# A second kept path of 544 tokens beside the one of 576 in a masked attention with residual

## The chip, the cores and the metric

The kernel runs on one core of a Trainium2 chip. The metric is the device time of one execution in microseconds (us). Three runs of the kernel before gave 808.4, 808.93 and 811.0 us; the median is 808.93 us.

In the profile, PE is TensorE (PEld its weight loads), DVE is VectorE, ACT is ScalarE, POOL is GpSimd and SP is the engine that issues most transfers. A "q" behind an engine's name (DVEq) means its instruction queue: branches, register loads and waits stand there.

## The reference

The input x has 8 batches of 512 features by 1024 tokens. A mask of 8 x 1024 ones and zeros says which tokens are kept. Each batch goes through one attention layer with 8 heads of 64 features, and its output is added to x:

```python
q = xt @ Wq.T                                  # queries, keys and values are the same
scores = scale * einsum('bhqd,bhkd->bhqk', qh, qh)
logits = (scores * cmask + (1.0 - cmask) * NEG) * rmask
attn = softmax(logits, axis=-1)
ctx = einsum('bhqk,bhkd->bhqd', attn, qh)
out = ctx @ Wo.T
x = x + transpose(out)
```

A masked key gets no weight. A masked query has all logits 0, so that its result is the mean of all values: one and the same row for all masked queries of a batch. The drawn mask keeps 505, 529, 523, 514, 519, 519, 533 and 521 tokens in the eight batches.

## The kernel before

**Two paths.** The kernel first ranks the kept tokens of each batch (`early`). `verdict` holds the largest number of kept tokens in any batch. Each engine loads it into a register (line 1255) and compares (line 1256): if it is below NK = 576, the short path (`late`) runs, which works on NK packed tokens a batch. Its column NK - 1 holds the mean token, which stands for all masked queries. After that path each engine loads `flag` (line 1259) and jumps over the general path for all 1024 tokens (line 1260), unless the short path was not taken or found a sum that vanishes.

**The packed tokens.** `gather` fetches the kept rows of x (turned to tokens by features and stored in DRAM as xd) by an indirect DMA on POOL's queue, five chunks a batch: four of 128 tokens and a last one of 64 (`sizes`, LAST = 4). `collect` turns them on TensorE into xc, with features on the partitions (line 527).

**Pairs.** The work goes by 32 pairs: 8 batches times 4 pairs of heads. For pair p the loop over the chunks c = 0 to 4 does this:

- `scores`: s = keys of the chunk times all queries, in two halves of KH = 288 queries for two heads (line 627), then the exponential e on ScalarE (line 631). In the last chunk of 64 keys the two halves of the queries share the 128 partitions.
- `add_up`: VectorE sums e over the valid queries (line 648). The scores are symmetric, so these sums are the softmax denominators.
- tasks for other pairs, put between the chunks by hand (`slots_of` and the tables TURN, SEARCH, LATER, FINISH): `project` of pair p + 2 (pq, line 558), `values` of pair p + 2 (transposes v, line 577, and the squared lengths, lines 585 to 594), `bias_of` of pair p + 1, the output projection of the batch before (`output`, line 777), `collect` of the next batch, transposes and searches of the next batch, and the last steps of an earlier one.

After the chunks, `attend` multiplies e with v (av, line 664). `invert` sends the sums through DRAM to get them as a row over all partitions (rb), and `contexts` multiplies. The order in which the code calls these functions is the order of the instructions on each engine; no scheduler moves them.

**The last chunk.** qT is 640 columns wide. Columns 576 to 639 are a copy of the last 64 (line 567), so that the last chunk also has 128 rows. In `output`, the last chunk of 64 rows is computed in two halves of 256 features, which lie in partitions 0 to 63 and 64 to 127 of one bank; two DMAs on POOL's queue store them (line 786).

**Homes.** At its end the kernel needs, for every token, the row of the packed output that belongs to it (`origin`; `placed` is the same as floats). `early` computes it from the ranks with five VectorE instructions (lines 1060 to 1065, tiles `home` and `wrap`), a transpose on TensorE (`home_t`, line 1077) and two copies (lines 1078 and 1079). `place_blocks`, in pair 2, chunk 2, makes `block_origin` of it (line 830).

**The end.** The last batch goes a shorter way (`begin_output`, `end_output`, `attend_last`, `fetch_last`, `finish_tokens`), and ACT's queue issues the last stores (line 897).

Of the kernel before, what the change touches and what calls it, by code (L numbers as in the profile page):

```python
# [11 lines left out]
I32 = mybir.dt.int32  # L12
# [9 lines left out]
Q = 32  # L22
NK = 576
TINY = 1e-26
# [3 lines left out]
def attention_of_all_tokens(ctx, tc, x, mask, out, ident, wqT, woT):  # L28

# [275 lines left out]
def attention_of_kept_tokens(ctx, tc, x, mask, wq, wo, out, ident, wqT, woT, verdict, flag):  # L319

    nc = tc.nc
# [10 lines left out]
    NQ = 4  # L355
    KH = NK // 2
    sizes = [min(P, NK - c * P) for c in range(-(-NK // P))]
    NC = len(sizes)
    LAST = NC - 1
    assert sizes[LAST] == DK == P // 2  # L360
    W = NC * P

    sb = ctx.enter_context(tc.tile_pool(name="fsb", bufs=2))
# [3 lines left out]

    count = keep.tile([P, NK], F32, name="count")
    quadrant = keep.tile([P, A], F32, name="quadrant")
# [10 lines left out]
    sums = [keep.tile([P, 2, NC], F32, name=f"sums_{i}") for i in range(2)]  # L380
    ris = [keep.tile([P, Q], F32, name=f"ris_{i}") for i in range(2)]
    ranks = dr.tile([B * NT, P], F32, name="ranks", bufs=1)

# [19 lines left out]
    def queries_of(b):  # L403

        valid = sb.tile([P, NK], F32, tag="valid", name=f"valid_{b}")
        nc.gpsimd.tensor_scalar(valid, count, kept[:, b : b + 1], None, ALU.is_lt)  # L406
        part = sb.tile([P, KH], F32, tag="part", name=f"part_{b}")
        for r in range(2):
            rows = slice(r * DK, (r + 1) * DK)
            nc.gpsimd.tensor_copy(part[rows, :], valid[rows, r * KH : (r + 1) * KH])  # L410
        valids[b] = valid, part

    def turn_first(i):

        r, at = divmod(i * P, NB)
        pt = bank(f"xt_0_{i}")
        for d in range(ND):
            nc.tensor.transpose(pt[:, d * P : (d + 1) * P], xs[0][r][:, d, at : at + P], ident)  # L418
        if i == 0:
            xds[0] = dr.tile([T, D], F32, tag="xd", name="xd_0")  # L420
        tag = "oc" if i < NC else "xin"
        xt = sb.tile([P, D], F32, tag=tag, name=f"xt_0_{i}", bufs=NC)
        nc.scalar.copy(
            xt.rearrange("p (a d f) -> p a d f", a=A, d=ND),
            pt.rearrange("p (d a f) -> p a d f", d=ND, a=A),
        )
        nc.gpsimd.dma_start(xds[0][i * P : (i + 1) * P, :], xt)

    def mean_first():
        xbars[0] = sb.tile([P, ND, NN], F32, tag="xbar", name="xbar_0")  # L430
        for r in range(NN):
            nc.vector.tensor_reduce(xbars[0][:, :, r], xs[0][r], axis=AX.X, op=ALU.add)

    def turn(b, i):

        n = T // NQ
        r, at = divmod(i * n, NB)
        if i == 0:
            xds[b] = dr.tile([T, D], F32, tag="xd", name=f"xd_{b}")
        xt = sb.tile([P, n // Q, P], F32, tag="xt", name=f"xt_{b}_{i}", bufs=2)
        nc.vector.transpose(  # L447
            xt.rearrange("p k (d f) -> p k d f", d=ND),
            xs[b][r][:, :, at : at + n].rearrange("p d (k t) -> p k d t", t=Q),
        )  # L450

        def store():
            for a in range(A):
                to = xds[b][i * n : (i + 1) * n, a * P : (a + 1) * P]
                nc.sync.dma_start(
                    to.rearrange("(k t) c -> t k c", t=Q), xt[a * Q : (a + 1) * Q, :, :]
                )

        stores[1].append(store)
# [20 lines left out]
    def place_ranks(b):  # L480
        rank = sb.tile([P, T], F32, tag="rank", name=f"rank_{b}", bufs=1)
        found = sb.tile([P, NC], F32, tag="found", name=f"found_{b}")
        source = sb.tile([P, NC], I32, tag="source", name=f"source_{b}")
        searches[b] = rank, found, source
# [8 lines left out]
    def search(b, i):  # L493

# [52 lines left out]
    def project(pair, hf):  # L549
# [16 lines left out]
        if hf == 1:  # L566
            nc.scalar.copy(qT[:, NK:W], pq[:, KH - DK : KH])

# [41 lines left out]
    def scores(pair, c):  # L610
        qT, nm = qTs[pair], "%d_%d_%d" % (*pair, c)
        heads = [slice(h * DK, (h + 1) * DK) for h in range(2)]
        keys = slice(c * P, c * P + sizes[c])
        if c < LAST:
# [133 lines left out]
    def sum_last(pair):  # L748

        rb = rbs[pair]  # L750
        end = rb[:, NK - DK : NK]
        nc.vector.tensor_tensor(end, end, rb[:, NK:W], ALU.add)
        nc.vector.tensor_tensor(lowest, lowest, end, ALU.min)
        nc.vector.tensor_scalar(end, end, TINY, None, ALU.max)
        nc.vector.reciprocal(end, end)
# [8 lines left out]
    ods, gs, xrs = {}, {}, {}  # L764
    places = [slice(DK + c * P, DK + (c + 1) * P) for c in range(LAST)] + [slice(0, DK)]

    def output(b, i):
# [4 lines left out]
        oc = sb.tile([P, D], F32, tag="oc", name=f"oc_{b}_{i}", bufs=NC)  # L772
        parts = 2 if i == LAST else 1
        w = D // parts
# [87 lines left out]
    def fetch_last(b):  # L862

        for i in range(NT):
            tag, bufs = ("xin", NC) if i < NC else ("g", NT)
            g = sb.tile([P, D], F32, tag=tag, name=f"g_{b}_{i}", bufs=bufs)
            rows = min(NK, DK + (i + 1) * P)
            nc.gpsimd.indirect_dma_start(
# [100 lines left out]
    def early():  # L969
# [11 lines left out]
        def where(t, src, pattern, op, base, mult):  # L981
# [13 lines left out]
            count,  # L995
            pattern=[[1, NK]],
            base=0,
# [33 lines left out]
        nc.scalar.copy(rank, pr[:BC, :P])  # L1031
        nc.gpsimd.dma_start(ranks, rank)

        place_ranks(0)
# [23 lines left out]

        home = keep.tile([BC, P], F32, name="home")
        nc.vector.tensor_scalar(home, rank, float(-NK), None, ALU.add)  # L1060
        nc.vector.tensor_tensor(home, home, mrow, ALU.mult)
        nc.vector.tensor_scalar(home, home, float(NK - 1 + DK), None, ALU.add)
        wrap = keep.tile([BC, P], F32, name="wrap")
        nc.vector.tensor_scalar(wrap, home, float(NK), float(-NK), ALU.is_ge, ALU.mult)
        nc.vector.tensor_tensor(home, home, wrap, ALU.add)
        nc.vector.memset(low, 1.0)
# [7 lines left out]
        for i in range(NC):  # L1074
            search(0, i)
        pt = bank("home_t")
        nc.tensor.transpose(pt[:, :BC], home, ident[:BC, :BC])
        nc.vector.tensor_copy(placed, pt[:, :BC].rearrange("p (b c) -> p b c", c=NT))
        nc.vector.tensor_copy(origin, placed)

    def late():
        weights["wq"] = order_columns(load_weights(wq, "wq"), "wq")
# [33 lines left out]
        for p, pair in enumerate(pairs):  # L1116
# [3 lines left out]
            for c in range(NC):  # L1120
# [36 lines left out]
                if pr == 2 and c == 0 and b > 0:  # L1157
                    fetch(b - 1)
                if p == 2 and c == 2:
                    place_blocks()  # L1160
# [60 lines left out]
def kernel(  # L1221
# [9 lines left out]

    nc = tc.nc
# [11 lines left out]
    with ExitStack() as pools:  # L1249
        early, late = attention_of_kept_tokens(  # L1250
            pools, tc, x, mask, wq, wo, out, ident, wqT, woT, verdict, flag
        )
        with tc.manual_schedule():
            early()
        fit = nc.values_load(verdict[0:1, 0:1], min_val=0, max_val=2 * T)
        with tc.If(fit < NK):
            with tc.manual_schedule():
                late()
    again = nc.values_load(flag[0:1, 0:1], min_val=0, max_val=1)
# [31 lines left out]
```

## Time and profile before

| what | value |
|---|---|
| median of the runs | 808.93 us |
| span of the profiled execution | 724.6 us |
| own time of the profiled execution beyond its span | not shown |
| median less span | 84.3 us |
| PE, DVE, ACT, POOL busy | 673.4, 542.0, 384.1, 171.9 us |
| one steady batch (av of one pair to the same av of the next batch) | 83.02 us |
| mean granted clock of TensorE | 0.980 |

The page of the profile gives busy times, the chain of work that ended last, and groups of instructions by line. A row of a group reads: line, engine, operation, tile written <- tiles read, shapes, count | busy us, mean ns of one | idle time of the engine just before them, and who ended it. A matmul in float32 counts as two instructions. Matmuls overlap, so the mean of one is longer than the distance from one to the next; the timeline gives the distance. A row of the timeline reads: start in us, length in us, engine, line, operation, tiles, shape, count, and in brackets the wait before it. A row of the table by stage reads: from:to, length, busy us of PE, PEld, DVE, ACT and POOL with counts, the granted clock of TensorE, the busy share of the DMA engines, and GB/s. A row of the view of one source line gives the shortest, median and longest duration in ns and the start of the first and the last in us.

### The profile page before, as it was taken

The numbers are of one execution on the slowest core, as the hardware profiler recorded it, in microseconds if no ns is written. First come the engines' busy times: TensorE is split into PE (matmuls) and PEld (weight loads), VectorE is DVE, ScalarE is ACT, GpSimd is POOL, SyncE is SP. The second block draws the span as 40 slices with busy tenths as digits, with TensorE's granted clock in tenths as the row PEclk, the third lists the DMA queues.
The fourth block names the chain that finished last, engine by engine and source line by source line (L and its number), as shares of the span: only waits on it lengthen the run. The fifth ranks groups of instructions, "written<-read, shape, count | busy, mean of one in ns | idle before, by whom it ended". The sixth has DMA issues, their size and how long they took to land.

```text
span 724.6 us, 11742 instructions
## 1 busy us (share of the span) xinstructions
PE 673.4 (93%) x4027; PEld 378.0 (52%) x4027; DVE 542.0 (75%) x1568; ACT 384.1 (53%) x763; POOL 171.9 (24%) x208
## 2 busy tenths in 40 slices
PE   6699999999999999999999999999999999998973
PEld 5555555555554555546554555455554555554332
DVE  6269967758986799858986699858988598637862
ACT  5476567455654556445664657445673645445300
POOL 4721000062102601054101701044100710023021
PEclk9899999999999999999999999999999999999985
DMA  8544152772579636783579634785468821754238
GB/s 292 157 150 129 56 164 64 185 196 93 181 199 234 201 96 181 209 207 124 164 193 229 200 125 142 206 222 152 164 169 199 215 88 41 167 132 131 59 113 248
DMA packets 96405, 117.35 MB, mean 162 GB/s; under 512 B 10080, under 2 KB 73632, under 8 KB 96336
## 3 DMA queue, kind: packets, MB, share of 16 engines
q1 hardware_dynamic: 79584, 74.14, 38.9%
q0 software_dynamic: 12528, 40.28, 17.8%
q10 hardware_dynamic: 4224, 2.10, 1.0%
q8 instruction: 33, 0.54, 0.3%
q14 instruction: 36, 0.29, 0.1%
HBM read 73.30 MB, written 43.18 MB: 161 GB/s over the span
## 4 chain that ended last, share of the span: by engine, by line
PE 82%; DVE 7%; ACT 6%; DMA 3%; issue 2%; POOL 0%; SPq 0%; DVEq 0%; POOLq 0%
PE av L664 19%; PE s L627 19%; PE pq L558 17%; PE po L777 15%; ACT e L631 4%; PE v L577 3%; PE xc L527 2%; DVE junk L648 2%; PE pa L797 2%; DVE junk L502 1%; DMA g<-od,origin 1%; PE xt L418 1%; DMA rb<-row 1%; PE po L813 1%; PE top L600 0%
## 5 line engine op out<-in xcount | busy, mean ns | idle before, releaser
L648 DVE CUSTOM_DVE_ANT_0 junk<-e,valid 128x576 f32<-128x576 f32 x256 | 193.5, 756 | 68.3 <-ACT e L631 61.3
L627 PE MATMUL s<-qT 64*128 64x288 f32 (+1 forms) x1280 | 186.7, 434 | 16.9 <-ACT e L631 16.7
L631 ACT ACTIVATE e<-s,bias 128x576 f32<-128x576 f32 x256 | 175.5, 737 | 20.4 <-PE s L627 17.2
L627 PEld LDWEIGHTS s<-qT 64*128 64x128 f32 (+1 forms) x1280 | 91.7, 174 | 103.9 <-ACT e L631 50.2
L558 PE MATMUL pq<-xc,wqT 128*128 128x288 f32 x512 | 140.4, 418 | 0.0
L664 PE MATMUL av<-e,v 128*64 128x288 f32 x1024 | 135.8, 411 | 0.1
L558 PEld LDWEIGHTS pq<-xc,wqT 128*128 128x128 f32 x512 | 92.2, 190 | 40.9 <-ACT cT L680 8.5
L777 PE MATMUL po<-woT,cT 128*128 128x512 f32 (+1 forms) x336 | 113.4, 525 | 0.0
L664 PEld LDWEIGHTS av<-e,v 128*64 128x64 f32 x1024 | 69.6, 136 | 55.0 <-ACT v L580 8.3
L786 POOL DMA_DIRECT2D od<-oc x42 | 23.4, 557 | 276.0 <-ACT oc L784 276.0
L777 PEld LDWEIGHTS po<-woT,cT 128*128 128x128 f32 (+1 forms) x336 | 48.9, 172 | 56.0 <-issue 51.5
L680 ACT COPY cT<-av 128x288 f32<-128x288 f32 x62 | 21.7, 402 | 97.7 <-PE av L664 97.7
L879 POOL DMA_INDIRECT g<-od,block_origin x56 | 62.1, 1109 | 19.0 <-issue 14.3
L784 ACT COPY oc<-po 128x512 f32<-128x512 f32 (+1 forms) x35 | 19.0, 543 | 87.0 <-PE po L777 85.7
L565 ACT COPY qT<-pq 128x288 f32<-128x288 f32 x64 | 25.5, 398 | 63.8 <-PE pq L558 63.8
L514 POOL DMA_INDIRECT xin<-xd,source x40 | 42.4, 1060 | 43.8 <-DVE m L603 25.6
L406 POOL TENSOR_SCALAR valid<-count,kept 128x576 f32<-128x576 f32 x8 | 14.1, 1762 | 130.3 <-DVE sums L648 130.2
L447 DVE STREAM_TRANSPOSE xt<-x 128x1024 f32<-128x1024 f32 x28 | 34.7, 1240 | 11.0 <-DMA xd<-xt 10.9
L587 DVE TENSOR_REDUCE len<-sq 128x10 f32<-128x640 f32 x32 | 25.8, 806 | 21.3 <-ACT sq L585 21.3
L502 DVE TENSOR_SCALAR_CACHE_REDUCE junk<-rank,key 128x1024 f32<-128x1024 f32 (+4 forms) x40 | 39.7, 994 | 1.5 <-ACT rank L1046 1.5
L849 DVE TENSOR_TENSOR xr<-o,xr 128x512 f32<-128x512 f32 x56 | 38.8, 692 | 1.9
L846 DVE STREAM_TRANSPOSE o<-g 128x512 f32<-128x512 f32 x56 | 39.3, 701 | 0.0
(139 smaller groups left out, 630.5 us busy)
## 6 DMA issues: line engine op xcount, KB each, us to landing
x<-in_x_dram SPq DMA_DIRECT2D x56, 256.0 KB
xd<-xt SPq DMA_DIRECT2D x112, 128.0 KB
xr<-in_x_dram SPq DMA_DIRECT2D x28, 512.0 KB
out_dram<-xr SPq DMA_DIRECT2D x24, 512.0 KB
rb<-row SPq DMA_DIRECT2D x60, 160.0 KB
od<-oc POOLq DMA_DIRECT2D x28, 256.0 KB, 4.0
rank<-ranks SPq DMA_DIRECT2D x6, 512.0 KB
xd<-xt POOLq DMA_DIRECT2D x8, 256.0 KB, 3.8
```

The lines of the kernel that those rows point to most:

```text
L447: nc.vector.transpose(xt.rearrange("p k (d f) -> p k d f", d=ND), xs[b][r][:, :, at : at + n].rearrange("p d (k t) -> p k d t", t=Q),)
L502: nc.vector.tensor_scalar(junk[:, :n], rank[:, i * P :], key[:, col], 0.0, ALU.is_le, ALU.add, accum_out=found[:, col])
L514: nc.gpsimd.indirect_dma_start(out=xin[:n, :], out_offset=None, in_=xds[b], in_offset=bass.IndirectOffsetOnAxis(ap=searches[b][2][:n, i : ...
L558: nc.tensor.matmul(pq[:, :KH], wqT[:, d, pr * P : (pr + 1) * P], xcs[b][:, d, cols], start=(d == 0), stop=(d == ND - 1),)
L627: nc.tensor.matmul(s[to, h, :KH], qT[heads[h], keys], qT[heads[h], queries], start=True, stop=True)
L631: nc.scalar.activation(e[:, hf if c < LAST else 0, :, :], s[:, :, :KH], AF.Exp, bias=biases[pair][:, c : c + 1], scale=SCALE,)
L648: nc.vector.tensor_tensor_reduce(junk[:, :n].rearrange("p (f k) -> p f k", k=KH), e[:, :, h, :], (valid if c < LAST else part).rearrange(" ...
L664: nc.tensor.matmul(av[head, :KH], v[keys, c, head], e[keys, hf if c < LAST else 0, h, :], start=(c == 0), stop=(c == LAST),)
L777: nc.tensor.matmul(po[k * n : (k + 1) * n, :w], cTs[b, pr][:, i * P : i * P + n], woT[:, pr, k * w : (k + 1) * w], start=(pr == 0), stop=( ...
L846: nc.vector.transpose(o.rearrange("p k t -> p (k t)"), gs[b, i])
L849: nc.vector.tensor_tensor(to, o, to, ALU.add)
L879: nc.gpsimd.indirect_dma_start(out=g, out_offset=None, in_=ods[b], in_offset=bass.IndirectOffsetOnAxis(ap=block_origin[:, b, i : i + 1], a ...
```

## The change

A second length, SHORT = 544, gets its own copy of the short path. `late` now takes the length and sets NK, KH, the chunk sizes and the places of the output rows by `fit_to`; its code stands twice in the program. With NK = 544 a half has 272 queries, the last chunk has END = 32 tokens, qT's columns 544 to 639 are three copies of the last 32, and the last chunk of an output is computed in four quarters of 128 features with four stores. The `home` instructions depend on NK, so they leave `early` and become `place_all`, called in pair 1, chunk 4, ahead of that chunk's tasks. xd, the feature sums and the source rows of batch 0 get buffers of their own, since both copies read them.

```diff
-NK = 576
+SHORT = 544
+LONG = 576
...
+    def fit_to(n):
+        nonlocal NK, KH, END
+        NK, KH, END = n, n // 2, n - LP
+        assert DK % END == 0
+        sizes[:] = [P] * LAST + [END]
+        places[:] = [slice(END + c * P, END + (c + 1) * P) for c in range(LAST)] + [slice(0, END)]
...
-            xds[0] = dr.tile([T, D], F32, tag="xd", name="xd_0")
+            xds[0] = dr.tile([T, D], F32, tag="xd_0", name="xd_0", bufs=1)
...
-            nc.scalar.copy(qT[:, NK:W], pq[:, KH - DK : KH])
+            nc.scalar.copy(
+                qT[:, NK:W].rearrange("p (r k) -> p r k", k=END),
+                pq[:, KH - END : KH].unsqueeze(1).to_broadcast([P, (W - NK) // END, END]),
+            )
...
-        keys = slice(c * P, c * P + sizes[c])
+        keys = slice(c * P, c * P + (P if c < LAST else DK))
...
-        end = rb[:, NK - DK : NK]
-        nc.vector.tensor_tensor(end, end, rb[:, NK:W], ALU.add)
+        end = rb[:, LP : LP + DK]
+        nc.vector.tensor_tensor(end, end, rb[:, LP + DK : W], ALU.add)
...
-        parts = 2 if i == LAST else 1
+        parts = P // n
...
-        home = keep.tile([BC, P], F32, name="home")
-        nc.vector.tensor_scalar(home, rank, float(-NK), None, ALU.add)
-        nc.vector.tensor_tensor(home, home, mrow, ALU.mult)
-        nc.vector.tensor_scalar(home, home, float(NK - 1 + DK), None, ALU.add)
-        wrap = keep.tile([BC, P], F32, name="wrap")
-        nc.vector.tensor_scalar(wrap, home, float(NK), float(-NK), ALU.is_ge, ALU.mult)
-        nc.vector.tensor_tensor(home, home, wrap, ALU.add)
...
+    def place_all():
+
+        BC = B * NT
+        mrow, rank = seen["mrow"], seen["rank"]
+        home, wrap = homes
+        nc.vector.tensor_scalar(home, rank, float(-NK), None, ALU.add)
+        nc.vector.tensor_tensor(home, home, mrow, ALU.mult)
+        nc.vector.tensor_scalar(home, home, float(NK - 1 + END), None, ALU.add)
+        nc.vector.tensor_scalar(wrap, home, float(NK), float(-NK), ALU.is_ge, ALU.mult)
+        nc.vector.tensor_tensor(home, home, wrap, ALU.add)
         pt = bank("home_t")
         nc.tensor.transpose(pt[:, :BC], home, ident[:BC, :BC])
         nc.vector.tensor_copy(placed, pt[:, :BC].rearrange("p (b c) -> p b c", c=NT))
         nc.vector.tensor_copy(origin, placed)
 
-    def late():
+    def late(n):
+        fit_to(n)
...
+                if p == 1 and c == 4:
+                    place_all()
                 if p == 2 and c == 2:
                     place_blocks()
...
-        with tc.If(fit < NK):
+        with tc.If(fit < SHORT) as short:
             with tc.manual_schedule():
-                late()
+                late(SHORT)
+        with short.Else():
+            with tc.If(fit < LONG):
+                with tc.manual_schedule():
+                    late(LONG)
```

More of the change, by code (lines that the diff above doesn't have):

```diff
@@ L355, in attention_of_kept_tokens @@
     NQ = 4
-    KH = NK // 2
-    sizes = [min(P, NK - c * P) for c in range(-(-NK // P))]
-    NC = len(sizes)
+    NC = -(-LONG // P)
     LAST = NC - 1
-    assert sizes[LAST] == DK == P // 2
+    LP = LAST * P
     W = NC * P
+    assert LP < SHORT < LONG == LP + DK and DK == P // 2
+    NK = KH = END = 0
+    sizes, places = [], []
+    def fit_to(n):
[4 more added lines that the diff above has]
+        places[:] = [slice(END + c * P, END + (c + 1) * P) for c in range(LAST)] + [slice(0, END)]
     sb = ctx.enter_context(tc.tile_pool(name="fsb", bufs=2))
@@ L366, in attention_of_kept_tokens @@
     keep = ctx.enter_context(tc.tile_pool(name="keep", bufs=1))
-    count = keep.tile([P, NK], F32, name="count")
+    count = keep.tile([P, LONG], F32, name="count")
     quadrant = keep.tile([P, A], F32, name="quadrant")
@@ L381, in attention_of_kept_tokens @@
     ris = [keep.tile([P, Q], F32, name=f"ris_{i}") for i in range(2)]
+    homes = [keep.tile([B * NT, P], F32, name=f"home_{i}") for i in range(2)]
+    seen = {}
     ranks = dr.tile([B * NT, P], F32, name="ranks", bufs=1)
@@ L405, in queries_of @@
         valid = sb.tile([P, NK], F32, tag="valid", name=f"valid_{b}")
-        nc.gpsimd.tensor_scalar(valid, count, kept[:, b : b + 1], None, ALU.is_lt)
+        nc.gpsimd.tensor_scalar(valid, count[:, :NK], kept[:, b : b + 1], None, ALU.is_lt)
         part = sb.tile([P, KH], F32, tag="part", name=f"part_{b}")
@@ L429, in mean_first @@
     def mean_first():
-        xbars[0] = sb.tile([P, ND, NN], F32, tag="xbar", name="xbar_0")
+        xbars[0] = keep.tile([P, ND, NN], F32, name="xbar_0")
         for r in range(NN):
@@ L482, in place_ranks @@
         found = sb.tile([P, NC], F32, tag="found", name=f"found_{b}")
-        source = sb.tile([P, NC], I32, tag="source", name=f"source_{b}")
+        if b:
+            source = sb.tile([P, NC], I32, tag="source", name=f"source_{b}")
+        else:
+            source = keep.tile([P, NC], I32, name="source_0")
         searches[b] = rank, found, source
@@ L764, in attention_of_kept_tokens @@
     ods, gs, xrs = {}, {}, {}
-    places = [slice(DK + c * P, DK + (c + 1) * P) for c in range(LAST)] + [slice(0, DK)]
     def output(b, i):
@@ L866, in fetch_last @@
             g = sb.tile([P, D], F32, tag=tag, name=f"g_{b}_{i}", bufs=bufs)
-            rows = min(NK, DK + (i + 1) * P)
+            rows = min(NK, END + (i + 1) * P)
             nc.gpsimd.indirect_dma_start(
@@ L995, in early @@
             count,
-            pattern=[[1, NK]],
+            pattern=[[1, LONG]],
             base=0,
@@ L1032, in early @@
         nc.gpsimd.dma_start(ranks, rank)
+        seen["mrow"], seen["rank"] = mrow, rank
         place_ranks(0)
```

## The prediction

> **What bounds the kernel now.** I read the page first: its span, the busy times, and the chain that ended last.
>
> ```profile
> span 724.6 us, 11742 instructions
> PE 673.4 (93%) x4027; PEld 378.0 (52%) x4027; DVE 542.0 (75%) x1568; ACT 384.1 (53%) x763; POOL 171.9 (24%) x208
> PE 82%; DVE 7%; ACT 6%; DMA 3%; issue 2%; POOL 0%; SPq 0%; DVEq 0%; POOLq 0%
> ```
>
> TensorE is busy for 93% of the span and carries 82% of the chain. The median of the runs is 808.93 us, so 84.3 us lie around the span; the profiled execution shows nothing of them, and I add changes of the span to the median. Next came the groups of instructions with shapes kept apart (count | busy us, mean ns), because the change alters shapes.
>
> ```profile
> L648 DVE CUSTOM_DVE_ANT_0 junk<-e,valid 128x576 f32<-128x576 f32 x256 | 193.5, 756 | 68.3 <-ACT e L631 61.3
> L627 PE MATMUL s<-qT 64*128 64x288 f32 x1024 | 163.8, 435 | 9.2 <-ACT e L631 9.0
> L558 PE MATMUL pq<-xc,wqT 128*128 128x288 f32 x512 | 140.4, 418 | 0.0
> L664 PE MATMUL av<-e,v 128*64 128x288 f32 x1024 | 135.8, 411 | 0.1
> L777 PE MATMUL po<-woT,cT 128*128 128x512 f32 x224 | 100.3, 595 | 0.0
> L648 DVE CUSTOM_DVE_ANT_0 junk<-el,part 128x288 f32<-128x288 f32 x64 | 29.0, 454 | 2.9 <-ACT el L631 1.7
> L565 ACT COPY qT<-pq 128x288 f32<-128x288 f32 x64 | 25.5, 398 | 63.8 <-PE pq L558 63.8
> L784 ACT COPY oc<-po 128x512 f32<-128x512 f32 x28 | 16.4, 585 | 77.9 <-PE po L777 77.9
> L527 PE MATMUL xc<-ident,xin 64*128 64x64 f32 x32 | 3.7, 235 | 0.0
> ```
>
> Every 288 here becomes 272 and every 576 becomes 544, if the new path is taken. The stage that repeats eight times is a batch, and one batch in the table of busy times by stage reads (engine busy us, matmuls in brackets):
>
> ```profile
> 253.21:336.23 83.02, 80.57 (x487) 44.36 (x488) 67.47 (x193) 46.57 (x95) 20.80 (x22) 1.00 0.65 177
> ```
>
> PE works 80.57 of 83.02 us and DVE 67.47, so in a steady batch PE is the bound and the other engines have slack. The spacing of its work is read from the timeline, from one group's start to the next.
>
> ```profile
> 285.75 4.10 PE L664 MATMUL av<-e,v 128*64 128x288 f32 x32
> 289.78 0.72 PE L664 MATMUL av<-el,v 64*64 64x288 f32 x8
> 290.43 1.24 PE L627 MATMUL s<-qT 64*128 64x288 f32 x8
> 291.60 2.21 PE L558 MATMUL pq<-xc,wqT 128*128 128x288 f32 x8
> 293.64 3.60 PE L777 MATMUL po<-woT,cT 128*128 128x512 f32 x8
> 297.17 1.24 PE L627 MATMUL s<-qT 64*128 64x288 f32 x8
> ```
>
> **Part 1, narrower queries (a gain on PE).** A pq of 288 columns takes (293.64-291.60)/8 = 255 ns, a po of 512 columns (297.17-293.64)/8 = 441 ns: 0.83 ns a column. From busy time, 100.3/224 and 140.4/512 give 448 and 274 ns, so 0.78. I take 0.80, and 16 columns fewer are 12.8 ns. The s take (291.60-290.43)/8 = 146 ns and the av (289.78-285.75)/32 = 126 ns, about half of a pq of equal columns: two run side by side, so a pair counts once. Slots: 512 pq, 1024/2 s, 1024/2 av; the last-chunk s and av (8 of each for each of 32 pairs of heads, 256) go 8 in 290.43-289.78 = 0.65 us, which reads as four abreast, 64 slots each. That is 1664 slots x 12.8 ns = 21.3 us. Ends: if an s pair (293 ns, more than one pq) is held by something other than columns, 1088 slots x 12.4 ns = 13.5 us; if the last chunk goes in pairs and a column costs 0.83, 1792 x 13.3 ns = 23.8 us.
>
> ACT and DVE shorten with it. ACT: (585-398)/224 = 0.83 ns a column, so two exponentials of a chunk lose 2 x 27 = 53 ns where PE's four s slots lose 51: the short waits of s for e stay as they are. DVE: (756-454)/288 = 1.05 ns a column, 34 ns off each of 32 add-ups of a batch, about 1.4 us off 67.5. The wider fill copy of qT (96 columns for 64) adds 32 x 27 ns = 0.9 us to ACT, which has more than 36 us of slack a batch.
>
> **Part 2, the last chunk of 32.** The last output of a batch, on PE's timeline:
>
> ```profile
> 308.73 5.48 PE L777 MATMUL po<-woT,cT 128*128 128x512 f32 x24
> 314.14 1.24 PE L627 MATMUL s<-qT 64*128 64x288 f32 x8
> ```
>
> It holds 8 full matmuls (3.53 us) and 16 of the last chunk, 5.41-3.53 = 1.88 us a batch. These become 32 matmuls of 128 columns, in four column strips. A slot costs 255-288x0.8 = 25 ns plus columns, so 127 ns. Four abreast, 8 slots, are 1.0 us, a gain of 0.85 us; two abreast, 16 slots, are 2.0 us, a loss of 0.15 us. I take four, since four 64*64 matmuls share a slot above: 7 batches x 0.85 = 6 us, ends +6 and -1. The page "TensorEngine Tiling (Array Packing)" of the Trainium skill, section Theoretical Speedup, allows 4x for a dimension of 32; by that rule the term is the same 6 us, but no row of this trace shows strips of 32 at work on long streams. The last transposes of xc go from 64 columns to 32: half of 3.7 us at most, taken as 0.5. On POOL's queue each such output issues four od stores for two:
>
> ```profile
> 314.92 1.06 POOL L786 DMA_DIRECT2D od<-oc  x2 [1.13 <-ACT oc L784]
> 316.43 1.58 POOL L514 DMA_INDIRECT xin<-xd,source  x1 [0.45 <-issue]
> 326.49 1.53 PE L527 MATMUL xc<-ident,xin 128*128 128x128 f32 x12
> ```
>
> That is 1.1 us more, and behind it stand the gathers xin and g of the next steps. PE wants the first xin 10 us after the first gather starts, so I cost it at nothing; if the cover is gone it is at most 1 us a batch, 7 us. Sum of parts 1 and 2: 21.3 + 6 + 0.5 = 28 us gained, ends 12 and 31.
>
> **Part 3, place_all moved into pair 1 (a loss).** The early copy leaves the start; it cost nothing there, for DVE later sits idle until ACT's rank. Its new place is between the scores of pair 1, chunk 4, and values of pair 3. PE executes in order, so its new transpose home_t waits there for DVE, and DVE is behind.
>
> ```profile
> 65.35 0.71 PE L627 MATMUL s<-qT 64*64 64x288 f32 x8 [0.36 <-ACT e L631]
> 65.99 0.76 PE L577 MATMUL v<-ident,qT 128*128 128x128 f32 x5
> 86.62 0.30 PE L577 MATMUL v<-ident,qT 128*128 128x128 f32 x1 [0.89 <-DVE m L602]
> 72.56 0.75 DVE L502 TENSOR_SCALAR_CACHE_REDUCE junk<-rank,key 128x512 f32<-128x512 f32 x1
> 73.42 0.81 DVE L587 TENSOR_REDUCE len<-sq 128x10 f32<-128x640 f32 x1
> 93.74 0.76 DVE L648 CUSTOM_DVE_ANT_0 junk<-e,valid 128x576 f32<-128x576 f32 x1 [2.41 <-ACT e L631]
> 47.00:66.00 19.00, 18.29 (x122) 10.55 (x120) 17.99 (x48) 13.86 (x31) 0.00 (x0) 1.00 0.51 129
> 6.96 0.21 DVE L1060 TENSOR_SCALAR home<-rank_row 64x128 f32<-64x128 f32 x1
> 8.03 0.28 DVE L1065 TENSOR_TENSOR home<-home,wrap 64x128 f32<-64x128 f32 x1
> ```
>
> PE reaches that point at 65.99. DVE, full in this stretch (17.99 of 19 us), ends the search of chunk 4, which precedes place_all in the code, only at 73.5. Then come the five home instructions, 6.96 to 8.31, so 1.35 us. In the new kernel PE comes about 1.4 us sooner (112 slots until then), DVE about 0.8 us (14 add-ups of 34 ns and an earlier start): 64.6 against 72.7 + 1.35 = 74.1. PE stands still for 9.5 us. Queued behind home_t are values of pair 3, all of attend and all of pair 2; ACT and then DVE wait for them. Little is won back: until DVE has caught up (idle before 93.74), PE waited for it only 0.89 us. And a PE that has stood still comes back slow:
>
> ```profile
> 15.00:19.00 4.00, 0.03 (x1) 0.00 (x0) 3.30 (x7) 3.73 (x5) 0.62 (x2) 1.00 0.78 300
> 23.00:26.00 3.00, 2.65 (x19) 2.62 (x13) 0.17 (x1) 1.17 (x2) 2.34 (x4) 0.50 0.77 195
> 26.00:30.00 4.00, 3.87 (x29) 3.27 (x29) 0.00 (x0) 3.40 (x7) 3.43 (x5) 0.99 0.22 83
> ```
>
> From 15 to 19 PE has 0.03 us of matmuls; from 23 to 26 it is busy again, but at a granted clock of 0.50, and only from 26 on at 0.99. Those 3 us at half speed lose 1.5 us; the phase can be longer, and I take 2 us, with 1.5 and 3.5 as ends. Part 3: 9.5 + 2.0 - 0.9 = 10.6 us lost; the two arrival times are good to about 2 us, so the ends are 8 and 14.
>
> **Part 4, the branches.** On entry the taken side falls through its compare (the first of each pair of L1256). At its end each engine jumps over the whole 576 path. Before, that jump crossed nothing; but the jump over the general path at L1260 shows what a long one costs.
>
> ```profile
> L1256 DVEq COMPARE_BRANCH  x2: 50/54/57, 22.1 to 717.6; - x2
> L1260 PEldq COMPARE_BRANCH  x1: 4027/4027/4027, 717.1 to 717.1; - x1
> L1260 DVEq COMPARE_BRANCH  x1: 73/73/73, 718.5 to 718.5; - x1
> L1260 DVEq EVENT_SEMAPHORE  x1: 21/21/21, 722.5 to 722.5; - x1
> ```
>
> TensorE's jump lasts 4.0 us, and DVE's next instruction stands 3.9 us behind its jump. DVE would now pay 3.9 us at 717.6 instead of 0.5, then the reading of the flag, then 3.9 us again: its end moves from 722.5 to about 725.9, +3.4 us on the path that ends the kernel. Ends: 0, if the new jump is fetched ahead, and 7.5, if an engine has first to see the last stores land (they end near 722.5 too).
>
> **Sum:** -28 + 10.6 + 3.4 = -14 us. The span goes to about 710.6 and the time to 808.9 - 14 = 795 us.
>
> **Rivals.** (a) The stall of part 3 is hidden, because DVE was the bound of that stretch and PE only ran ahead. For it speaks DVE's full stretch, against it the single 0.89 us for which PE waited. It would give 808.9 - 28 + 3.4 = 784 us. (b) PE's matmuls are held by weight loads or starts rather than by columns: gain 12, time 808.9 - 12 + 14 = 811. Against it stand the 441 and 255 ns. (c) Slower than before: the 84.3 us around the span grow with the stored program, which gains a second path as long as the one that ran. If the general path is twice as long as that one, three units stand in 84.3 us, and a fourth adds up to 28 us: 823 us. It decides from a growth of 16 us; nothing in the profile speaks for growth, or excludes it. The Trainium skill's page "Runtime: NRT & Kernel Launch" (The launch sequence and Model-switch cost) has about 15 us per launch and about 70 us for a change of program, neither a function of length; by it the growth is nothing, and no run here shows it. (d) The new path isn't taken. The drawn mask keeps 505 to 533 tokens a batch, all below 544, so only other inputs would do it: then no gain, and 808.9 + 10.6 + 3 = 823 us.
>
> **Chances.** Forecast 0.62, (a) 0.18, (b) 0.07, (c) 0.11, (d) 0.02. A measurement can tell about 0.3%, 2.4 us, so faster means below 806.5. Forecast and (a) are nearly all faster (0.79), and so is a small growth under (c) (0.02): 0.81. Within 0.3%: 0.07, from (b) and the middle of (c). Slower: 0.12, from (c), (d) and the tail of (b). The range takes in (a) below and the bad ends of parts 2 and 3 above, 782 to 807; what stays out is (b), (c) and (d).
>
> **What would show it.** Groups with 272 and 544 columns in the old counts; a steady batch near 79.5 us instead of 83.0; a PE wait of 9 to 10 us on DVE at home_t near 64 us, with granted clock 0.5 behind it; po of 128 columns, 32 a batch, in about 1 us; two gaps of near 4 us at the end where there was one. I would be wrong if PE waits for DVE at home_t for less than 4 us, if the batch shrinks by less than 2 us, or if time minus span moves by more than 3 us.

## The result and the profile after

The changed kernel takes 782.13 us (median of four executions, 777.81 to 786.09), the kernel before 809.62 us (median of four as well). The ratio is 0.966 (95% interval 0.961 to 0.971): 27.5 us saved, twice the 14 us of the forecast. The sign was right, the size was not. The time lies at the very edge of the range of 782 to 807 us, which the prediction had stretched that far down for rival (a), a mechanism that did not occur.

The page of the profile after, to be laid beside the page lines shown of before:

```profile
span 776.8 us, 11988 instructions
PE 668.4 (86%) x4139; PEld 387.6 (50%) x4139; DVE 533.5 (69%) x1568; ACT 378.6 (49%) x763; POOL 171.4 (22%) x222
PEclk9797999988999799996999999999999789998985
PE 79%; ACT 7%; DVE 5%; issue 3%; another core or an unknown queue 2%; DMA 2%; POOL 1%; DVEq 0%; POOLq 0%
```

The span did not shrink. It is 52 us longer than the 724.6 us of before, although the kernel is faster, and the execution that it belongs to took 778.75 us, only 2 us more than its span. TensorE is busy for 5 us less than before (668.4 for 673.4 us) but only for 86% of the span, and a new entry stands in the chain: waits ended by "another core or an unknown queue". So the profile of before and its times cannot come from executions of the same kind, and the 84.3 us that I put around the span are not there. One of the prediction's own signs of being wrong, time minus span moving by more than 3 us, has come up: it went from 84.3 to 2.

The groups by shape say that the new path ran (count | busy us, mean ns of one | idle before):

```profile
L622 DVE CUSTOM_DVE_ANT_0 junk<-e,valid 128x544 f32<-128x544 f32 x256 | 185.1, 723 | 97.8 <-ACT e L605 79.6 <-issue 12.4
L601 PE MATMUL s<-qT 64*128 64x272 f32 x1024 | 168.6, 444 | 48.9 <-ACT e L605 37.1 <-issue 11.7
L529 PE MATMUL pq<-xc,wqT 128*128 128x272 f32 x512 | 136.4, 410 | 4.7 <-issue 3.7 <-DVE m L576 1.0
L638 PE MATMUL av<-e,v 128*64 128x272 f32 x1024 | 130.2, 401 | 0.4
L750 PE MATMUL po<-woT,cT 128*32 128x128 f32 x224 | 7.6, 276 | 0.0
```

Every count is the old one with 272 and 544 columns. pq and av got shorter; s did not (444 ns for 435), and the idle time ahead of it rose from 9.2 to 48.9 us. (These means hold matmuls at a lower granted clock; in the changed kernel's run on a quiet chip, below, s takes 422 ns and the idle time is 9.4 us.) The view of waits (who waits <- for what: us in all, times, the longest) names what came new:

```profile
PE s L601 <- ACT e L605: 44.8, 55, 5.6
ACT e L605 <- remote: 17.3, 10, 6.4
DVE xc L515 <- remote: 12.8, 2, 6.4
PE home_t L1054 <- DVE home L1052: 8.8, 1, 8.8
```

The last line is the stall of part 3, near its forecast. The first three are something else: waits of up to 5.6 and 6.4 us, where scores had waited 0.4 us at most before. "remote", in two of them, says that the profile finds nothing on this core that ended just before the wait did; by its own times, what the engine waited for had long been done.

### The profile page after: what moved, and what is told of

It reads as the page before. It is cut to its first block, busy times and chain, and to the rows that moved or that the text cites. A ratio compares the mean times of both kernels' runs of the same rounds, so it can differ in the third digit from the quotient of the medians.

```text
span 776.8 us, 11988 instructions
## 1 busy us (share of the span) xinstructions
PE 668.4 (86%) x4139; PEld 387.6 (50%) x4139; DVE 533.5 (69%) x1568; ACT 378.6 (49%) x763; POOL 171.4 (22%) x222
## 4 chain that ended last, share of the span: by engine, by line
PE 79%; ACT 7%; DVE 5%; issue 3%; another core or an unknown queue 2%; DMA 2%; POOL 1%; DVEq 0%; POOLq 0%
PE s L601 20%; PE av L638 18%; PE pq L529 16%; PE po L750 13%; ACT e L605 5%; PE xc L498 3%; PE v L551 2%; PE pa L770 2%; DVE junk L622 1%; DVE junk L473 1%; DMA g<-od,origin 1%; PE xt L393 1%; PE po L786 1%; PE mean L512 1%
## 5 line engine op out<-in xcount | busy, mean ns | idle before, releaser
L622 DVE CUSTOM_DVE_ANT_0 junk<-e,valid 128x544 f32<-128x544 f32 x256 | 185.1, 723 | 97.8 <-ACT e L605 79.6
L601 PE MATMUL s<-qT 64*128 64x272 f32 (+1 forms) x1280 | 190.6, 438 | 56.6 <-ACT e L605 44.8
L605 ACT ACTIVATE e<-s,bias 128x544 f32<-128x544 f32 x256 | 170.8, 712 | 64.2 <-PE s L601 33.8
L529 PE MATMUL pq<-xc,wqT 128*128 128x272 f32 x512 | 136.4, 410 | 4.7 <-issue 3.7
L638 PE MATMUL av<-e,v 128*64 128x272 f32 x1024 | 130.2, 401 | 0.4
L529 PEld LDWEIGHTS pq<-xc,wqT 128*128 128x128 f32 x512 | 93.7, 193 | 40.1 <-issue 11.2
L750 PE MATMUL po<-woT,cT 128*128 128x512 f32 (+1 forms) x448 | 107.4, 436 | 0.0
L759 POOL DMA_DIRECT2D od<-oc x56 | 29.9, 536 | 273.4 <-ACT oc L757 272.4
L654 ACT COPY cT<-av 128x272 f32<-128x272 f32 x62 | 21.4, 388 | 101.2 <-PE av L638 79.9
L852 POOL DMA_INDIRECT g<-od,block_origin x56 | 57.3, 1022 | 18.9 <-issue 15.5
L757 ACT COPY oc<-po 128x512 f32<-128x512 f32 (+1 forms) x35 | 18.3, 522 | 81.4 <-PE po L750 81.4
L536 ACT COPY qT<-pq 128x272 f32<-128x272 f32 x64 | 24.7, 386 | 60.4 <-PE pq L529 57.2
L381 POOL TENSOR_SCALAR valid<-count,kept 128x544 f32<-128x544 f32 x8 | 13.5, 1693 | 177.4 <-DVE sums L622 177.3
L417 DVE STREAM_TRANSPOSE xt<-x 128x1024 f32<-128x1024 f32 x28 | 34.7, 1240 | 13.6 <-DMA xd<-xt 13.5
```

The costliest lines, as they stand in the source:

```text
L417: nc.vector.transpose(xt.rearrange("p k (d f) -> p k d f", d=ND), xs[b][r][:, :, at : at + n].rearrange("p d (k t) -> p k d t", t=Q),)
L529: nc.tensor.matmul(pq[:, :KH], wqT[:, d, pr * P : (pr + 1) * P], xcs[b][:, d, cols], start=(d == 0), stop=(d == ND - 1),)
L601: nc.tensor.matmul(s[to, h, :KH], qT[heads[h], keys], qT[heads[h], queries], start=True, stop=True)
L605: nc.scalar.activation(e[:, hf if c < LAST else 0, :, :], s[:, :, :KH], AF.Exp, bias=biases[pair][:, c : c + 1], scale=SCALE,)
L622: nc.vector.tensor_tensor_reduce(junk[:, :n].rearrange("p (f k) -> p f k", k=KH), e[:, :, h, :], (valid if c < LAST else part).rearrange(" ...
L638: nc.tensor.matmul(av[head, :KH], v[keys, c, head], e[keys, hf if c < LAST else 0, h, :], start=(c == 0), stop=(c == LAST),)
```

## The experiments

Twelve runs were made on three chips, each beside runs of the kernel before on the same chip. The theories that the expectations weigh are given in their own words there. I call a chip quiet where the kernel before takes about 728 us.

### The kernel before once more: e0_before_again

No edit. 

> The kernel before, unchanged, to see a second profiled execution of it. Theory A (the reasons of the prediction): the profiled execution shows what the timed ones do; span again near 724.6 us, some 84 us around it, no gap of TensorE over 3 us between 30 and 690 us. Theory B (formed from the profile after, where time less span is 2 us): the first profiled execution of the kernel before was not a typical one; a typical one has a span near 807 us, and the missing 82 us are gaps in pair 2 of the batches, where the scores wait for ACT although PE had long computed them.

Measured: 728.79 us (ten executions), the runs of before beside it 727.68 us, ratio 1.0018 (0.9999 to 1.0036), span of the profiled execution 728.0 us and its own time 729.76 us. On this chip the kernel before takes 81 us less than where the first times were taken, and time and span differ by 1.8 us. So the 84.3 us are, as far as the runs can tell, the difference of two chips: the profile that I was shown came from one like this (its batch of 83.02 us is 82.95 us here), the times from another. Which chips those were is not on record. What the 84.3 us consist of is shown by the last six runs; the terms of the sum are first tested here, where they can be read undisturbed.

### The home instructions earlier: e1_home_early

```diff
...
+    def turn_homes():
...
+                if p == 0 and c == 2:
+                    place_all()       # the five VectorE instructions alone
                 if p == 1 and c == 4:
-                    place_all()
+                    turn_homes()      # transpose and two copies
```

> The changed kernel with the five home instructions of VectorE called in pair 0, chunk 2; the transpose home_t and the two copies stay in pair 1, chunk 4. Theory A: the wait of 8.84 us at home_t and the slow clock behind it vanish, so 9 to 11 us less than the changed kernel: 771 to 773 us against 782. Theory B: the same wait vanishes, but other gaps move by several us too, so anything from 762 to 782 us. Rival of A (a of the prediction, DVE is the bound of that stretch): under 3 us less.

Measured: 707.36 us, ratio 0.973 (0.971 to 0.976). TensorE's timeline (start, length) has no wait left at the transpose:

```profile
65.62 0.69 PE L601 MATMUL s<-qT 64*64 64x272 f32 x8 [0.38 <-ACT e L605]
66.24 0.27 PE L1058 MATMUL home_t<-ident,home 64*128 64x64 f32 x1
66.44 0.76 PE L551 MATMUL v<-ident,qT 128*128 128x128 f32 x5
```

The expectation of 9 to 11 us was missed by the medians: the changed kernel takes 715.51 us on the other quiet chip (below; 0.9 us of it belong to that chip), so that the early homes gain 7.3 us there. The two profiled executions differ by 10.6 us (spans of 714.5 and 703.9 us), and 10.1 of these lie between the last av of pair 0 and that of pair 2, which are 46.8 us apart in the one and 36.7 in the other. The four executions of this run spread over 4.5 us, and the profiled one is the shortest. Rival (a), under 3 us, is out either way. The stall comes from the place of five short instructions in VectorE's order, and most of it goes with them.

### One kept path of 544 alone: e2_one_path

```diff
-        with tc.If(fit < SHORT) as short:
+        with tc.If(fit < SHORT):
             with tc.manual_schedule():
                 late(SHORT)
-        with short.Else():
-            with tc.If(fit < LONG):
-                with tc.manual_schedule():
-                    late(LONG)
```

> The changed kernel with only the path of 544; the 576 path and the Else are left out. Theory A: the second long jump at the end vanishes, 3.4 us less than the changed kernel, 778 to 779 us, and time less span does not move. Rival c of the prediction (a longer program costs around the span): more than 8 us less, and time less span falls. Theory B adds nothing, but its gaps can blur the 3.4 us.

Measured: 711.49 us, ratio 0.978 (0.976 to 0.981). The wait at home_t is there, 8.91 us. The last VectorE instruction ends 6.6 us ahead of the span's end; with both paths in the program it is 9.7 us in the run before this one and 10.9 in the next but one. Time less span is 1.8 us here and 1.8 and 1.9 us there, so rival (c) finds nothing that grows with the program.

### The path of 576 alone, with the moved homes: e3_long_alone

```diff
-        with tc.If(fit < SHORT) as short:
-            with tc.manual_schedule():
-                late(SHORT)
-        with short.Else():
-            with tc.If(fit < LONG):
-                with tc.manual_schedule():
-                    late(LONG)
+        with tc.If(fit < LONG):
+            with tc.manual_schedule():
+                late(LONG)
```

> The code of the changed kernel with only the path of 576: the narrower tiles, the last chunk of 32 and the second branch are undone, the moved home instructions stay. Theory A: the kernel before plus the wait at home_t, 819 to 821 us; the changed kernel less this one is then the part of the narrower tiles and the branch, -25 us by the prediction, or about -38 us if 782 is right. Theory B: the gaps in pair 2 stand here too, and their sum differs from that of the kernel before by up to 20 us either way.

Measured: 739.06 us, ratio 1.015 (1.013 to 1.017): part 3 by itself costs 11.4 us against a forecast of 10.6. The stretch behind the wait, by stage (from:to, length, busy us of PE, PEld, DVE, ACT, POOL, granted clock):

```profile
70.00:80.20 10.20, 4.12 (x18) 2.44 (x20) 7.21 (x24) 1.49 (x3) 3.87 (x4) 0.51 0.36 112
```

The clock is at 0.51 over the wait and some microseconds behind it. Against the run before (711.49 us, the same but for 544 in place of 576) this gives parts 1 and 2 by themselves: 27.6 us; the forecast was 28.

### The changed kernel once more: e4_after_again

No edit; another chip, on which the kernel before takes 728.57 us. 

> The changed kernel, unchanged, beside the kernel before on another chip. Theory A (my terms were right for executions without the gaps in pair 2; the gaps belong to one chip or its neighbours): where the kernel before takes about 728 us, this takes 714 to 716 us, a gain of 12 to 14 us, and its batches last 79.4 us each. Theory B (the gaps belong to this kernel's two paths, which give TensorE 1093 signalling matmuls for 666): its batches last 83 us and more on every chip, 740 us or more.

Measured: 715.51 us, ratio 0.982 (0.980 to 0.985), 13.1 us saved. The forecast of 14 us holds on this chip. By parts, from the four runs on these two chips (the second has the kernel before 0.9 us higher, which is taken off): -27.6 + 11.4 + 3.1 = -13.1 us. The last term, this run less the one with one path, is part 4; 3.4 were forecast. Taken as steps from kernel to kernel the three terms add up by themselves; what is tested is each against its forecast.

### Both repairs together: e5_home_early_one_path

The edits of the second and the third experiment in one kernel. 

> The changed kernel with the home instructions in pair 0, chunk 2, and with the path of 544 alone. Theory A: the run with one path (711.5) less the stall of 11.4 us, plus about 1 us because VectorE is full in that stretch: 701 us where the kernel before takes 728. Against the run with two paths and early home instructions (707.4) that is 6.4 us less, of which 3.1 us are the longer end and the rest the 0.1 us a batch and the first batches. Rival (the two paths cost nothing but the jump): 704 us.

Measured: 702.14 us, ratio 0.964 (0.963 to 0.965): the best version, though inputs with 544 to 575 kept tokens would take its general path. Here the early homes gain 10.2 us on the run with one path. Of those that keep both paths, the one with early homes is best. That one less this one is 6.1 us, 3 us more than the 3.1 us of the jump. The profiled executions differ by less, 4.3 us: 2.9 behind the last VectorE instruction and 1.4 ahead of it. Where the other 2 us of the medians come from was not followed.

### The unchanged kernels on a third chip: e8_before_third and e7_after_third

No edit; one execution each, on a chip where the kernel before takes 810.61 us. 

> The kernel before, unchanged, for a profile beside the two others. Where it takes 809 us: gaps in pair 2 of nearly all batches that sum to about 80 us, with releases of TensorE that come microseconds late, although it has only 666 signalling matmuls. Where it takes 728 us: none.

 

> The changed kernel, unchanged, as the companion of the run without indirect fetches. 714 to 716 us where the kernel before takes 728; 778 to 786 us where it takes 809, with gaps in pair 2 of most batches.

Measured: 808.39 and 791.46 us, spans 806.7 and 789.7 us. The second was expected at 778 to 786 us and is above that. On this chip the change therefore gains 17 to 19 us, not 27.5. Time and span differ by 1.7 us here too, so the 81 us between chips lie inside the span. Where, the table by stage tells. One batch of the kernel before, cut at the last av of pairs 1 and 2, first on the quiet chip, then on this one:

```profile
156.45:175.46 19.01, 18.35 (x133) 10.91 (x131) 14.56 (x39) 11.48 (x22) 10.15 (x10) 1.00 0.54 165
175.46:239.40 63.94, 62.15 (x357) 33.38 (x355) 52.73 (x154) 35.02 (x72) 9.91 (x13) 1.00 0.68 182
```

```profile
155.70:186.96 31.26, 21.93 (x133) 12.76 (x131) 15.91 (x47) 12.10 (x22) 9.51 (x10) 0.78 0.33 101
186.96:250.90 63.94, 62.15 (x357) 33.39 (x355) 51.39 (x146) 35.01 (x72) 9.99 (x13) 1.00 0.68 182
```

Three quarters of the batch agree to 0.01 us. All of the 12.25 us lies in the stage of pair 2, with the same 133 matmuls and a clock of 0.78 instead of 1.00: TensorE is idle for 8.7 us more (9.33 for 0.66) and busy for 3.6 us more. The same cut for the changed kernel, first on the quiet chip of the run above, then in the profile after:

```profile
162.91:181.24 18.33, 17.68 (x133) 10.91 (x131) 13.03 (x37) 11.17 (x22) 10.83 (x11) 1.00 0.60 179
181.24:242.32 61.08, 59.20 (x372) 33.14 (x370) 52.65 (x156) 34.17 (x72) 9.90 (x14) 1.00 0.68 180
```

```profile
162.80:193.70 30.90, 23.06 (x133) 14.22 (x131) 15.72 (x47) 11.47 (x22) 10.35 (x11) 0.78 0.33 106
193.70:254.78 61.08, 59.20 (x372) 33.12 (x370) 50.19 (x146) 34.17 (x72) 9.98 (x14) 1.00 0.69 187
```

Again only pair 2 differs. Inside it, GpSimd's row of instructions, then ScalarE's, then TensorE's, all from the profile after (in brackets the wait before, and who ended it):

```profile
164.87 0.87 POOL L485 DMA_INDIRECT xin<-xd,source  x1 [0.31 <-issue]
166.05 0.95 POOL L852 DMA_INDIRECT g<-od,block_origin  x1 [0.30 <-issue]
...
175.06 1.14 POOL L852 DMA_INDIRECT g<-od,block_origin  x1 [0.30 <-issue]
```

```profile
170.97 0.71 ACT L605 ACTIVATE e<-s,bias 128x544 f32<-128x544 f32 x1 [1.44 <-PE s L601]
178.08 1.32 ACT L605 ACTIVATE e<-s,bias 128x544 f32<-128x544 f32 x2 [6.39 <-remote]
```

```profile
171.74 1.28 PE L601 MATMUL s<-qT 64*128 64x272 f32 x4 [0.88 <-issue]
172.95 2.52 PE L498 MATMUL xc<-ident,xin 128*128 128x128 f32 x12
178.85 2.18 PE L601 MATMUL s<-qT 64*128 64x272 f32 x8 [3.38 <-ACT e L605]
```

GpSimd issues thirteen gathers in one go, five xin and eight g, from 159.2 to 176.2. TensorE's scores start at 171.74 and end at 173.02; ScalarE, which needs them, starts only at 178.08, 5.1 us later, and TensorE then waits 3.38 us for ScalarE. The trace's semaphore updates can be matched to the matmuls that send them, one after another. In the profile after, 18 of 1093 updates are not recorded, so this is an estimate: of 1072 that were matched, 89 come over 0.5 us behind their matmul's end, 7.7 us at most and 268 us in all, and all but one of them lie in the stretches of a batch in which g gathers are issued. The first two bursts, of five xin alone, show none. In the changed kernel on the quiet chip it is none of 1090. GpSimd's own instructions are no longer for it: the 56 g take 57.3 us here and 62.6 us there. The transfers aren't either: 0.33 of 30.90 and 0.60 of 18.33 us are 10 and 11 us.

### The gathers of g replaced by plain transfers: e6_g_plain, e9_before_g_plain, e10_after_g_plain

That the gathers cause the delay is, so far, only that they stand beside it. In these three kernels (the changed one, once with one execution and once with two, and the kernel before) the 56 gathers of g become plain transfers from SP's queue, which leaves out the reordering of the output rows:

```diff
-            nc.gpsimd.indirect_dma_start(
-                out=g,
-                out_offset=None,
-                in_=ods[b],
-                in_offset=bass.IndirectOffsetOnAxis(
-                    ap=block_origin[:, b, i : i + 1], axis=0
-                ),
-            )
+            nc.sync.dma_start(g, ods[b][0:P, :])
```

> The changed kernel with the 56 indirect fetches g of GpSimd's queue replaced by plain transfers of the same size on SP's queue; it leaves out the reordering of the output rows of the first seven batches. On a chip where the kernel before takes about 728 us both theories give 714 to 718 us, since TensorE's releases come at once there. On a chip where it takes about 809 us: Theory B1 (TensorE's releases are held up by GpSimd's indirect transfers, which fill the first half of pair 2) gives 715 to 735 us, with no release over 1 us late; Theory B2 (they are held up by something outside the kernel, whenever it comes) gives 770 to 790 us as for the changed kernel.

 

> The kernel before with the 56 indirect fetches g replaced by plain transfers on SP's queue; it leaves out the reordering of the output rows of the first seven batches. On a chip where the kernel before takes 809 us, Theory B1: 735 to 745 us, most of the 80 us gone, a rest for the indirect transfers xin. Where it takes 728 us: 726 to 730.

 

> The same replacement in the changed kernel, for the difference of the two. Theory B1: without the fetches g the change gains 12 to 16 us on any chip, as the terms of the prediction say; the larger gain where the kernel before takes 809 us came out of the gaps. Rival (the change gains 27 us there for another reason, such as a faster narrow matmul): the difference of the two stays at 25 us or more there.

Measured, all on the third chip: the changed kernel 725.32 us where it took 791.46 us with the gathers, and 726.14 us when repeated, ratio to the kernel before 0.897 (0.881 to 0.913); the kernel before 741.88 us where it took 809.33, ratio 0.917 (0.907 to 0.926). The stage of pair 2 in the first of the three:

```profile
162.73:184.23 21.50, 19.13 (x132) 12.00 (x130) 15.68 (x47) 11.60 (x22) 2.32 (x3) 0.92 0.46 152
```

It falls from 30.90 to 21.50 us, with the five xin gathers still issued at 159 to 166 us. Taking 56 gathers off GpSimd's queue wins 67 us for the kernel before and 66 us for the changed one (791.46 to 725.32), more than their own time on GpSimd, 57.3 us. The delays are not all gone: both kernels stay 10 to 14 us above their times on the quiet chips, and by the same matching 17 of TensorE's signals still come over 0.5 us late, 2.3 us at most, where none over 1 us was expected. Without the g gathers the change is worth 741.88 - 726.14 = 15.7 us, near the 13.1 of the quiet chip and not the 27.5 of the result; the 2.6 us between are of the size of the delays that are left. So the surplus of the result belongs to the delays in the gathers' stage, and not to a term of the sum.

### Early homes on the chip with delays: e11_home_early_again

The edit of the second experiment. 

> The changed kernel with the home instructions of VectorE in pair 0, chunk 2. Where the kernel before takes 728 us: 707 us again. Where it takes 809 us: the changed kernel (778 to 791) less about 8 us, 770 to 785, since the gaps of pair 2 stay.

Measured: 779.36 us, ratio 0.963 (0.954 to 0.972). It is 12 us under the one execution of the changed kernel on this chip (791.46), and 72 us over its own 707.36 on the quiet one. One execution is little to compare with where the changed kernel's delays vary, but the profiles are plain: from the last av of pair 0 to that of pair 2 it is 36.7 us for 46.7, as on the quiet chips. The repair of part 3 keeps its worth here, and does nothing against the delays.

## Why the prediction was wrong

**The working of the parts held.** On the chips without delays each term can be read, and each is near. Part 1 and 2: the steady batch was forecast at 79.5 us and is 18.33 + 61.08 = 79.41; of the 3.54 us less than before, 0.68 lie in the stage of pair 2 and 2.86 in the rest. The last output chunk in four strips was forecast at 1.0 us. The last output on TensorE's timeline, in the changed kernel on the quiet chip:

```profile
230.85 4.61 PE L750 MATMUL po<-woT,cT 128*128 128x512 f32 x40
235.39 1.19 PE L601 MATMUL s<-qT 64*128 64x272 f32 x8
```

The 40 matmuls hold it for 4.54 us, of which 3.53 are the eight full ones; 32 strips in 1.01 us. So of the two values that I weighed, the strips do run four abreast. The two added od stores of each such output cost nothing that shows on the quiet chip: the stage of pair 2, which holds the gathers behind them, got shorter.

**Part 3** was forecast as TensorE standing from 64.6 to 74.1, with 2 us for the clock. TensorE, VectorE and the table by stage in the same run:

```profile
64.82 0.69 PE L601 MATMUL s<-qT 64*64 64x272 f32 x8 [0.38 <-ACT e L605]
74.35 0.37 PE L1054 MATMUL home_t<-ident,home 64*128 64x64 f32 x1 [8.84 <-DVE home L1052]
```

```profile
72.02 0.75 DVE L473 TENSOR_SCALAR_CACHE_REDUCE junk<-rank,key 128x512 f32<-128x512 f32 x1
72.88 0.21 DVE L1048 TENSOR_SCALAR home<-rank_row 64x128 f32<-64x128 f32 x1
74.01 0.28 DVE L1052 TENSOR_TENSOR home<-home,home 64x128 f32<-64x128 f32 x1
```

```profile
69.00:70.00 1.00, 0.00 (x0) 0.00 (x0) 0.97 (x4) 0.00 (x0) 0.62 (x1) 0.76 0.85 229
78.00:79.00 1.00, 1.00 (x6) 0.48 (x6) 0.93 (x5) 0.00 (x0) 0.00 (x0) 0.50 0.07 16
79.00:80.00 1.00, 1.00 (x8) 0.56 (x6) 0.90 (x8) 0.00 (x0) 0.00 (x0) 0.62 0.00 0
80.00:81.00 1.00, 1.00 (x12) 0.60 (x10) 0.31 (x3) 0.00 (x0) 0.00 (x0) 1.00 0.00 0
```

VectorE ends the search at 72.77 and the homes at 74.29, within 0.2 us of what was worked out. TensorE comes at 65.5 for the 64.6 that I had, and stands for 8.84 us in place of 9.5. Its clock falls within the slice from 69 to 70, four microseconds into the wait, and is back within the slice from 79 to 80: TensorE works about 5.4 us at half clock, which loses 2.7 us. The sum, 11.5, leaves nothing won back of the 0.9 us that I took off; the path of 576 with moved homes measured 11.4. Rival (a), the hidden stall, is out, though 784 us was the nearest number to the result: the right size from a mechanism that did not occur.

**Part 4.** The branch behind the taken path, the reading of the flag and the second branch, in the changed kernel on the quiet chip (shortest/median/longest in ns, first and last start):

```profile
L1231 PEldq COMPARE_BRANCH  x2: 86/2229/4372, 13.6 to 701.8; - x2
L1231 DVEq COMPARE_BRANCH  x2: 50/54/57, 21.3 to 703.0; - x2
L1238 DVEq TENSOR_LOAD <-flag x1: 331/331/331, 707.5 to 707.5; - x1
L1239 PEldq COMPARE_BRANCH  x1: 4709/4709/4709, 706.7 to 706.7; - x1
```

TensorE pays 4.4 and then 4.7 us; VectorE's next instruction stands 4.5 us behind its first jump. The two gaps that were forecast are there, and the end is 3.1 us later. The Trainium skill's page "Runtime: NRT & Kernel Launch", section Instruction fetch mechanics, says that a taken branch whose target lies outside the window that is loaded waits for its code to be fetched; the rows agree with that, and give it a size that the page doesn't have. That it is the fetch which takes the time is not shown by a run here.

**The step that failed is the first one of the sum, its base:** "The median of the runs is 808.93 us, so 84.3 us lie around the span; the profiled execution shows nothing of them, and I add changes of the span to the median." Time less span is 1.7 to 2.0 us wherever both belong to one execution. The 82 us lay inside executions like those that were timed, in the stages with gathers, and the profile that I argued from shows none of them. The change moved these delays too, and the sum had no term for that. Rival (c), which let those 84.3 us grow with the program, falls with the same step. A gap of a tenth of the time between a profile and its times should have been read as a sign that the profile was of another kind of execution; I wrote a rival for it growing, and none for it lying inside.

**What made 13 into 27.** Compared with the quiet chips, the delays cost the kernel before 81 us and the changed one 67 us in the result (782.13 less 715.51) and 76 us on the third chip. In the profile after, cut at the last av of pairs 1 and 2, the stages of pair 2 last 30.9, 31.2, 31.5, 23.1, 22.1 and 30.5 us, and the shorter one of the last batch 16.9; on the quiet chip they last 18.3 and 11.2. Two of the six got off with 4 to 5 us of delay, where the kernel before loses 12 to 13.5 in each of its six and 6.6 in the last. Summed, the delays of these stages are 82 us for the kernel before on the third chip and 65 us in the profile after: the 17 us between them cover the 14.4 by which the result exceeds the quiet chip's 13.1. On the third chip one of the changed kernel's stages lasts 25.6 and one 28.1 us, the others 30.6 to 33.4; the delays sum to 77.5 us, and the gain there is smaller to match. So it is shown that the surplus comes from there, and shown, by the plain transfers, that it goes with the g gathers. Its size is no fixed worth of the change: the gain was 27.5 us in the result and 17 to 19 on the third chip. Not settled is why some stages of the changed kernel get off lightly (a shift of the gathers against the scores would do it, but no run varied only that), why one chip delays TensorE's signals and another does not, and whether it is the indirect form, GpSimd's queue or the reading of the index that does the harm, since the plain transfers change all three. What the same edit does on a chip without delays was not run.

## What to carry to other kernels

Before adding a forecast change to a measured time, ask whether profile and times agree: a profiled execution that is a tenth shorter than the median is of another execution, and the missing part is inside the kernel until shown otherwise. A step that is moved "to where its inputs are known" has to be placed by the in-order engine that is furthest behind: five instructions of 1.4 us behind VectorE's backlog stopped TensorE for 8.8 us, and a place one pair earlier gave back 10 of the 11 us that they cost in the profiles. When a gain differs between chips, cut a steady batch at the same matmuls on both and compare the stages: here 64 of 83 us agreed to 0.01 us, and the remaining stage held the whole difference of the batch.

## What the runs showed of the hardware

- In the profile after, TensorE's signals reach the other engines up to 7.7 us late while GpSimd issues a burst of thirteen gathers; the stage goes from 18.3 to 30.9 us, and its granted clock, with the waits that it now has, from 1.00 to 0.78. The third chip shows the same stage at the same clock. Two of the chips used show none of it with the same program (728.8 and 728.6 us for 808 to 811).
- Replacing 56 gathers, 57 us of GpSimd's time, by plain transfers on SP's queue shortened the kernel by 66 to 67 us on such a chip: what an engine that is busy for 22% of the span issues can set the time of the others, though which property of the gathers does it is open.
- The clock fell about 4 us into a wait of TensorE and came back 5.4 us after its work did; in the runs with the path of 544 alone and of 576 alone it came back 5.9 and 4.4 us after. The Trainium skill's page "TensorE: Matmul & The Clock Gate", Part 1, gives at least one idle window of about 3.4 us for the first and at least one busy window of about 3.4 us for the second, with a window that runs freely. Both agree with these traces: none of the times is below 3.4 us.
- TensorE's two jumps over code that isn't run last 4.4 and 4.7 us, and VectorE's next instruction stands 4.5 us behind its first (rows of part 4). A program with one kept path more pays for one more of them at its end: 3.1 us.
